# A two-stage mixture-of-experts block: the second stage scatters into the output under an index bound, and its last tile stands under a condition

## The chip, the core and the metric

The kernel runs on one core of a Trainium2 chip. The metric is the device time of one execution in microseconds (us), taken as the median of several runs. All data are 32-bit floats.

## The reference

The input x has 4 batches of 512 rows with 256 columns, 2048 rows in all. Three residual steps follow each other, each on a layer-normalised x:

```python
x = x + 0.5 * ffn(layernorm(x), gate, w0, w1, wo)      # stage one
x = x + attn(layernorm(x), ...)                        # 16 heads, low-rank q and kv, rotary part
x = x + 0.5 * ffn(layernorm(x), gate, w0, w1, wo)      # stage two, the same weights

def ffn(x, gate, w0, w1, wo):                          # 8 experts, the 2 best for each row
    top_w, top_i = top_k(x @ gate, 2)
    combine = one_hot(top_i) weighted by softmax(top_w)
    inter = silu(x @ w0[e]) * (x @ w1[e])              # 256 -> 512, for each expert e
    return sum over e of combine[e] * (inter @ wo[e])  # 512 -> 256
```

So each row goes through two of the eight experts in each stage, and 4096 (row, expert) pairs have to be computed in a stage.

## The kernel before, in words

**Tiles.** The pairs of a stage are sorted by expert into tiles of 128 rows. As the counts are known at run time alone, the number of tiles is the worst case: `NTILES` is 36 for every input. An expert's remainder of at most 64 rows takes half a tile, which it shares with another expert's; the first four places of the second list of tiles (`NSHARED`) can be such shared tiles. Slots that no row fills point at spare rows behind the 2048 real ones, or have weight zero.

**Lists.** A stage's tiles come in two lists that `list_tiles` makes. In stage two the first, `list_a`, has 17 tiles that are certainly full once three of the four batches are routed. The second, `list_b`, has the other 19 and is made after the last batch is routed, while the tiles of `list_a` run. Small matmuls with selection matrices (`sel`) pick out each tile's row numbers (`idx`), weights (`w`) and the offset of its expert in the weight tiles (`off`). `rest_of` lets shared and other tiles alternate for the first eight places, so the tiles 17 to 24 hold four shared tiles, and the tiles 25 to 35 are whole ones.

**One tile** goes through these steps in `ffn_tiles`: `gather` (POOL, indirect DMA) fetches its rows of the normalised x; `turn` transposes them on TensorE (`pt_x`) and copies them (`xT`, DVE); `hidden` loads the expert's offset into a register of TensorE (L1075), multiplies by w0 and w1 (`h`, L1104), takes the silu on ScalarE (`g`) and the product on DVE (`it`); `turn_hidden` transposes that (`pt_i`, `iT`); `project` multiplies by wo (`py`) and scales by the weight on DVE (`yo`, L1176); `scatter` (POOL, L1153) adds the rows of `yo` into DRAM by an indirect DMA that accumulates. The loop runs these one tile apart, so that TensorE has the next tile's product to do while the other engines work; gathers run two to four tiles ahead. Only the last tile has no follower: there the tile before it is projected between the two halves of the last hidden product.

**Scatters.** A row may lie in two tiles, so each scatter waits until the one before has landed. A shared tile scatters each half by itself, the second half one tile later (`later`). Each scatter is one instruction on POOL's queue, in which the gathers stand as well, in the program's order.

**Accumulators.** There are two DRAM tensors, `acc_d[0]` for stage one and `acc_d[1]` for stage two, each with 256 spare rows; POOL's queue clears the spare rows at the start (`clear`). Stage one adds into `acc_d[0]`, which starts as a copy of x. Attention reads it back, batch by batch, and when a batch is done `finish_x` writes it to `acc_d[1]` (SP's queue, L1469). Stage two's tiles 0 to 24 add into `acc_d[1]`. After tile 24 (`final` is 25) SP copies `acc_d[1]` into the output in four DMAs (L1192), which wait for tile 24's scatter; the tiles 25 to 35 add straight into the output. Their scatters wait for the four copies. The first two of them are held back (`HELD`) so that gathers can pass them on POOL's queue.

**Order.** The order of instructions on each engine is the one written in the program (`manual_schedule`); semaphores are put in by what reads and writes what. At the program's end (L1688) each engine drains and they meet at a barrier.

Of the kernel before, what the change touches and what calls it, by code (L numbers as in the profile page):

```python
# [42 lines left out]
def kernel(  # L43
# [64 lines left out]


    xn_d = [dp.tile([NTOK + P, D], F32, name=f"xn_d{f}") for f in range(2)]  # L110
    acc_d = [dp.tile([NTOK + 2 * P, D], F32, name=f"acc_d{f}") for f in range(2)]


    tab_d = [dp.tile([P * P, 2], F32, name=f"tab_d{f}") for f in range(2)]
# [2 lines left out]
    def rows(t, b):  # L117
        return t[b * S : (b + 1) * S, :].rearrange("(t p) d -> p t d", p=P)
# [95 lines left out]
    nc.gpsimd.memset(zero, 0.0)  # L214

    def clear():
        for t in (xn_d[0], acc_d[0], xn_d[1], acc_d[1]):
            for r in range(NTOK, t.shape[0], P):
                nc.gpsimd.dma_start(t[r : r + P, :], zero)
        for t in tab_d:  # L220
            nc.gpsimd.dma_start(t.rearrange("(c s) v -> c (s v)", s=P), zero)
# [656 lines left out]
    def list_tiles(ph, n, m, split=0, read=None):  # L878
# [14 lines left out]
        def parts():  # L893
# [95 lines left out]
            if last:  # L989
                for i, second in enumerate((tab2, ph.tab[:, 1, :HP])):  # L990
                    for r in (slice(0, HP), slice(HP, P)):
                        nc.tensor.matmul(
                            px[r, i, :ns], lhsT=ph.tab[:, i, r], rhs=sel[:, :ns],
                            start=True, stop=(r.start == 0),
                        )
                    nc.tensor.matmul(
                        px[HP:, i, :ns], lhsT=second, rhs=sh[:, 1], start=False, stop=True
                    )
                nc.tensor.matmul(
                    px[:1, 2, n : n + ns], lhsT=e_off, rhs=own, start=True, stop=True  # L1000
                )
            nc.tensor.matmul(
                px[:, 0, n0:n1], lhsT=ph.tab[:, 0, :], rhs=sel[:, n0:n1],
                start=True, stop=True,
# [24 lines left out]
            res["w"] = rt.tile([P, NTILES], F32, tag=f"wt{last}", name="wt")  # L1029
            nc.vector.tensor_copy(res["w"][:, :n], px[:, 1, :n])  # L1030
            res["off"] = rt.tile([1, NTILES], I32, tag=f"off{last}", name="off")
            n2 = n + n0
            nc.vector.tensor_copy(res["off"][:, :n2], px[:1, 2, :n2])
            if last:
                res["off2"] = res["off"][:, n:n2]

        return res, parts()

    HELD = 2
    flat_out = out.rearrange("b s d -> (b s) d")  # L1040

    def ffn_tiles(f, jobs, final=None):
# [2 lines left out]

        n = len(jobs)
        xg, xT, begun = {}, {}, set()

        def gather(j):
# [91 lines left out]
        def turn_hidden(it):  # L1143
# [4 lines left out]
            nc.scalar.copy(iT, pt)  # L1148
            return iT

        def scatter(these):
            for dst, idx, y in these:
                nc.gpsimd.indirect_dma_start(  # L1153
                    out=dst,
                    out_offset=bass.IndirectOffsetOnAxis(ap=idx, axis=0),
                    in_=y,
                    in_offset=None,
                    compute_op=ALU.add,
                )
            these.clear()  # L1160

        def project(j, off, iT):
            res, i = jobs[j]
            py = ps_p.tile([P, D], F32, tag="p", name="py")
            two = shared(j)
            for m in range(MC):
                first_half(two, py, iT[:, m, :], w_sb[2][:, bass.ds(off + m * D, D)], m, MC)
                if two:
                    wo = copies[j][2 * DC + m // 2][:, m % 2 * D : (m % 2 + 1) * D]
                    second_half(py, iT[:, m, :], wo, m, MC)  # L1170
            copies.pop(j, None)
            direct = final is not None and j >= final

            pool, tag = (qp, "q") if direct else (ptp, "pt")
            y = pool.tile([P, D], F32, tag=tag, name="yo")
            nc.vector.tensor_scalar_mul(y, py, res["w"][:, i : i + 1])  # L1176
            two_rows = P if two else 0
            dst = flat_out if direct else acc_d[f][: res["rows"] + two_rows, :]
            idx = res["idx"][:, i : i + 1]
            if two:  # L1180

                held.append((dst, half_idx[:, 0, i : i + 1], y))
                later.append((dst, half_idx[:, 1, i : i + 1], y))
            else:
                held.append((dst, idx, y))
            if not direct or j >= final + HELD:
                scatter(held)
            if final is not None and j == final - 1:

                for r in range(0, NTOK, NTOK // 4):  # L1190
                    r = slice(r, r + NTOK // 4)
                    nc.sync.dma_start(  # L1192
                        flat_out[r, :].rearrange("(p r) d -> p (r d)", p=P),
                        acc_d[f][r, :].rearrange("(p r) d -> p (r d)", p=P),
                    )

        held, later = [], []
        gather(0)
        gather(1)
        yield -1  # L1200
# [3 lines left out]
        for j in range(n):  # L1204
            gather(j + 2)
            if final is not None and j >= final:

                gather(j + 3)
                if j > final:
                    gather(j + 4)  # L1210
            scatter(later)
            if j == n - 1:

                off, it = hidden(j, lambda: project(*todo))
                todo = None
            else:
                off, it = hidden(j)
            yield j
            turn(j + 1)
            yield j  # L1220
            if todo is not None:
                project(*todo)
            yield j
            todo = (j, off, turn_hidden(it))
            yield j
        project(*todo)

# [236 lines left out]
    def finish_x(i):  # L1466
        b, h = items[i]
        if h == NH - 1:
            nc.sync.dma_start(rows(acc_d[1], b), xs[b])  # L1469

    def rest_of(res, n):

# [24 lines left out]
    for half in range(2):  # L1497
# [2 lines left out]

    nc.sync.dma_start(mark_d, list_a["w"][:, :n_a])
    nc.sync.dma_start(
        acc_d[0][:NTOK, :].rearrange("(p r) d -> p (r d)", p=P),
        x.rearrange("b s d -> (b s) d").rearrange("(p r) d -> p (r d)", p=P),
    )
    load_attention()
# [9 lines left out]
    for j in tiles:  # L1516
        place = place + 1 if place < 4 else 1
        beside.at(place)
        if j < n_a - 2:
            beside.step(3)  # L1520
            if j == n_a - 3 and place == 4:
                beside.finish()
        elif j == done + 1 and place == 1:
            load_x(0, rows(acc_d[0], 0))
        elif j == done + 2 and place == 1:
            beside.add(prepare(0), put_queries(0), put_queries(1))
        elif j > done + 2:
            beside.step(2 if place % 2 == 0 else 1)
        if j == len(jobs) - 1:
            if place == 1:  # L1530
                beside.finish()
            put_scores(place - 1)
            put_divide(place - 1)
    load_x(1, rows(acc_d[0], 1))
    for k in range(NT, NT + LEAD):
        put_scores(k)
        put_divide(k)
# [19 lines left out]
    for i, (b, h) in enumerate(items):  # L1557
        if h == 2:
            if b > 0:
                load = None  # L1560
                if b + 1 < B:
                    load = lambda b=b: load_x(b + 1, rows(acc_d[0], b + 1))
                routed = {}
                beside.add(route_one(two, b - 1, routed, load))
            if b + 1 < B:
                beside.add(prepare(b + 1))
            if b > 0:
                beside.add(scatter_one(two, routed))
            if b == B - 1:
                beside.add(listing)  # L1570
        for kc in range(NT):

            at = NT * (h % 2) + kc
            beside.at(at, at in (6, 7, 0, 1), LITTLE if late and ROOM[at] < 1.0 else ROOM[at])
            k = (i + 1) * NT + LEAD + kc
            if at != 1 or i == 0:
                put_scores(k)
            if at == 0 and i > 0:

                put_scores(k + 1)  # L1580
                put_weigh(i - 1, range(NT))
                put_divide(k)
                beside.step(PARTS[at])
            if at == 5:

                put_divide(k - 1)
            pts[i, kc] = turn_probs(probs[i], kc)
            for f in late:
                f()
            late.clear()  # L1590
            if at == 1:
                asked.add(put_queries(i // 2 + 2))
                beside.step(PARTS[at])
            elif at == 4 and h % 4 == 1 and i > 1:
                late.append(put_out(i - 2, 0))
            elif at == 6 and h % 4 == 1 and i > 1:
                late.append(put_out(i - 2, 1))
                late.append(lambda i=i: finish_x(i - 2))
            asked.step(ASKED[at])
            if at == 0 and i == 0:  # L1600
                put_divide(k)
            if at > 1 or at == 0 and i == 0:
                beside.step(PARTS[at])
        probs.pop(i)
# [87 lines left out]
```

## Time and profile before

| what | value |
|---|---|
| median of 3 runs | 1111.03 us (1108.27 to 1111.64) |
| the profiled execution | 1107.51 us, span of its instructions 1105.7 us |
| mean granted TensorE clock | 0.990 of full speed |
| TensorE (PE) busy | 1053.1 us, 95% of the span |
| DVE, ScalarE (ACT), POOL busy | 562.1, 476.5, 586.7 us |
| stage two's scatters | 40: 21 whole and 8 half ones to the accumulator, 11 to the output |
| the four copies to the output | issued from 1040.5 us on, 512 KB each, median 5.6 us to landing |

Times in the profile are counted from the span's first instruction. Busy time leaves out what an engine's sequencer does by itself (waits, register loads, branches, drains). A POOL row for an indirect DMA shows the time of its issue; the transfer goes on after it. A wait for several semaphores is put down to the one that came last, and "issue" means that the profile shows no wait. [...]

### The profile page before, as it was taken

The page shows a single profiled execution, that of the slowest core. Times are in us where ns is not written, and L with a number is a line of the kernel's source. Part 1 is how long each engine was busy: PE and PEld are TensorE (multiplying, and loading weights), DVE is VectorE, ACT ScalarE, POOL GpSimd, SP SyncE. Part 2 cuts the span into 40 slices and gives each one's busy share as a digit, 9 for nine tenths or more (in the row PEclk, how much of TensorE's full clock was granted, in tenths as well). Part 3 has the DMA queues.
Part 4 walks back from the last instruction along what each step waited for, and adds up shares of the span by engine and source line. Part 5 has one row for each costly group of instructions (what it writes and reads, how often), then busy time and mean ns, then how long its engine had stood idle before and what let it go on. Part 6 is the DMA issues. An engine that isn't in the chain of part 4 may idle for free. (4 is left out here: it accounts for less than half of the span.)

```text
span 1105.7 us, 14702 instructions
## 1 busy us (share of the span) xinstructions
PE 1053.1 (95%) x4738; PEld 598.2 (54%) x4738; DVE 562.1 (51%) x1329; ACT 476.5 (43%) x1030; POOL 586.7 (53%) x655
## 2 busy tenths in 40 slices
PE   4899999999999999999999999999999899999994
PEld 3566555666545555455455545554555566655662
DVE  6563222334566565676666766666855342322221
ACT  3622432222555556545565554556545231144120
POOL 4345455466556555536774546864574247444442
PEclk8999999999999999999999999999999999999998
DMA  9973233322100000100000100001000224223422
GB/s 315 366 189 48 45 49 52 67 34 39 34 1 1 1 1 1 58 1 1 1 2 20 39 1 1 1 1 39 2 6 1 86 50 45 45 48 53 129 44 24
DMA packets 44043, 53.57 MB, mean 48 GB/s; under 512 B 10720, under 2 KB 36704, under 8 KB 43872
## 3 DMA queue, kind: packets, MB, share of 16 engines
q0 software_dynamic: 16960, 22.07, 12.6%
q1 hardware_dynamic: 26736, 30.55, 8.6%
q8 instruction: 40, 0.66, 0.2%
q14 instruction: 35, 0.29, 0.1%
q10 hardware_dynamic: 272, 0.01, 0.0%
HBM read 34.74 MB, written 22.07 MB: 51 GB/s over the span
## 5 line engine op out<-in xcount | busy, mean ns | idle before, releaser
L1104 PE MATMUL h<-w_sb,xT 128*128 (+1 forms) x576 | 260.3, 594 | 2.5 <-DVE xT L1072 1.9
L1355 PE MATMUL ps<-k,q 128*128 128x512 f32 x512 | 259.8, 600 | 0.8 <-ACT pr L1365 0.8
L1363 DVE TENSOR_REDUCE nm<-ps 128x1 f32<-128x512 f32 x256 | 175.0, 687 | 74.6 <-PE ps L1355 70.1
L1365 ACT ACTIVATE pr<-ps,nm 128x512 f32<-128x512 f32 x210 | 144.2, 687 | 129.0 <-DVE nm L1363 101.7
L1372 POOL TENSOR_SCALAR pr<-pr,sm 128x512 f32<-128x512 f32 x210 | 142.4, 694 | 69.8 <-DVE sm L1370 68.5
L1140 DVE TENSOR_TENSOR it<-g,h 128x512 f32<-128x512 f32 x72 | 49.5, 688 | 221.2 <-PE h L1104 174.6
L1104 PEld LDWEIGHTS h<-w_sb,xT 128*128 128x128 f32 (+1 forms) x576 | 100.4, 184 | 109.6 <-issue 103.4
L1378 PEld LDWEIGHTS pt<-ident,pr 128*128 128x128 f32 x840 | 102.9, 141 | 103.7 <-issue 64.8
L1153 POOL DMA_INDIRECT acc_d<-yo,idx x53 | 83.9, 1582 | 140.3 <-DVE yo L1176 73.7
L1148 ACT COPY iT<-pt_i 128x512 f32<-128x512 f32 x72 | 42.3, 587 | 246.0 <-PE pt_i L1146 246.0
L1378 PE MATMUL pt<-ident,pr 128*128 128x128 f32 x840 | 135.5, 275 | 4.2 <-ACT pT L1385 3.8
L1104 PE MATMUL py<-w_sb,iT 128*128 (+1 forms) x576 | 136.9, 381 | 1.4 <-ACT iT L1148 1.4
L1391 PE MATMUL po<-pT,low 128*64 128x512 f32 x512 | 116.9, 598 | 4.7 <-ACT pr L1365 4.6
L1383 DVE COPY pT<-pt 128x512 f32<-128x512 f32 x128 | 87.4, 683 | 55.0 <-PE pt L1378 55.0
L1241 POOL TENSOR_TENSOR tsin<-tsin,sin_sb 128x512 f32<-128x512 f32 x36 | 46.5, 1293 | 126.1 <-DVE tsin L1239 123.9
L1104 PEld LDWEIGHTS py<-w_sb,iT 128*128 128x128 f32 (+1 forms) x576 | 100.5, 184 | 18.2 <-ACT iT L1148 2.4
L1355 PEld LDWEIGHTS ps<-k,q 128*128 128x128 f32 x512 | 82.4, 190 | 44.1 <-issue 19.4
L1057 POOL DMA_INDIRECT xg<-xn_d,idx x72 | 72.4, 1006 | 30.1 <-issue 15.6
L1385 ACT COPY pT<-pt 128x512 f32<-128x512 f32 x128 | 74.1, 579 | 15.3 <-PE pt L1378 15.3
L1391 PEld LDWEIGHTS po<-pT,low 128*64 128x64 f32 x512 | 33.9, 136 | 83.5 <-issue 56.5
L1137 ACT ACTIVATE g<-h 128x512 f32<-128x512 f32 x72 | 43.0, 597 | 59.2 <-PE h L1104 56.2
L1176 DVE TENSOR_SCALAR yo<-py,wt 128x256 f32<-128x256 f32 x72 | 34.8, 483 | 63.6 <-PE py L1104 55.4
(234 smaller groups left out, 1329.2 us busy)
## 6 DMA issues: line engine op xcount, KB each, us to landing
w_sb<-in_L_ffn_w_kernel_dram SPq DMA_DIRECT2D x8, 1024.0 KB, 13.7
w_sb<-in_L_ffn_wo_kernel_dram SPq DMA_DIRECT2D x5, 1024.0 KB, 14.5
xn_d<-xn SPq DMA_DIRECT2D x12, 256.0 KB, 4.3
x<-_attn_hidden_states_dram SPq DMA_DIRECT2D x4, 512.0 KB, 10.1
x<-acc_d SPq DMA_DIRECT2D x4, 512.0 KB, 3.9
acc_d<-x SPq DMA_DIRECT2D x4, 512.0 KB, 3.0
out_dram<-acc_d SPq DMA_DIRECT2D x4, 512.0 KB, 5.6
xg<-xn_d,idx POOLq DMA_INDIRECT x72, 2.8
```

The lines of the kernel that those rows point to most:

```text
L1057: nc.gpsimd.indirect_dma_start(out=xg[j], out_offset=None, in_=xn_d[f][: res["rows"], :], in_offset=bass.IndirectOffsetOnAxis(ap=res["idx" ...
L1104: nc.tensor.matmul(to[r], lhsT=lhsT[:, r], rhs=rhs, start=(k == 0), stop=(k == last - 1))
L1140: nc.vector.tensor_mul(it, g, ph[1])
L1153: nc.gpsimd.indirect_dma_start(out=dst, out_offset=bass.IndirectOffsetOnAxis(ap=idx, axis=0), in_=y, in_offset=None, compute_op=ALU.add,)
L1355: nc.tensor.matmul(ps, lhsT=qT[:, t * P : (t + 1) * P], rhs=st[b]["k"][h % 2], start=True, stop=True,)
L1363: nc.vector.tensor_reduce(nm, ps, AX.X, ALU.max, negate=True)
L1365: nc.scalar.activation(pr, ps, AF.Exp, bias=nm, accum_out=sm[:, t : t + 1])
L1372: nc.gpsimd.tensor_scalar(pr, pr, sm[:, t : t + 1], 1.0, ALU.mult, ALU.mult)
L1378: nc.tensor.transpose(pt[:, t * P : (t + 1) * P], probs[t][:, kc * P : (kc + 1) * P], ident)
L1383: nc.vector.tensor_copy(s, pt)
L1385: nc.scalar.copy(s, pt)
L1391: nc.tensor.matmul(po[j * RANK : (j + 1) * RANK], lhsT=st[b]["low"][:, kc, 1, :], rhs=pts[j], start=(kc == 0), stop=(kc == NT - 1),)
```

## The change

Stage two adds to the output from its first tile on. `finish_x` writes each finished batch to the output, `acc_d[1]` is gone with its clears, and so are the four copies and the holding back of scatters. As the output has no spare rows, every scatter of stage two carries a bound on the index: a row number above 2047 is left out and is no error. The loop runs over 35 tiles. The 36th, the last place of `list_b`, follows under a condition: one more matmul in `list_tiles` adds up the last column of `sel`, which is 1 if that place has rows and 0 if not, and the result stands in `off`'s row as one more element (`used`). After its last instruction of tile 34 each of the five engines loads `used` into a register and branches. In the branch that is taken when it is 0, an engine only brings the semaphores to the counts that the left-out tile would have given them. The matmul is there in both stages' `list_b`; the condition in stage two alone.

```diff
-    acc_d = [dp.tile([NTOK + 2 * P, D], F32, name=f"acc_d{f}") for f in range(2)]
+    acc_d = dp.tile([NTOK + 2 * P, D], F32, name="acc_d")
...
     def clear():
-        for t in (xn_d[0], acc_d[0], xn_d[1], acc_d[1]):
+        for t in (xn_d[0], acc_d, xn_d[1]):
...
+                nc.tensor.matmul(
+                    px[:1, 2, n + ns : n + ns + 1], lhsT=ones[:, :1], rhs=sel[:, n - 1 :],
+                    start=True, stop=True,
+                )
...
-            n2 = n + n0
+            n2 = n + n0 + (1 if last else 0)
             nc.vector.tensor_copy(res["off"][:, :n2], px[:1, 2, :n2])
             if last:
-                res["off2"] = res["off"][:, n:n2]
+                res["off2"] = res["off"][:, n : n2 - 1]
+                res["used"] = res["off"][:, n2 - 1 : n2]
...
     def ffn_tiles(f, jobs, final=None):
-        n = len(jobs)
+        n = len(jobs) - (0 if final is None else 1)
...
+        skip = {"bounds_check": NTOK - 1, "oob_is_err": False} if f else {}
+
         def scatter(these):
             for dst, idx, y in these:
                 nc.gpsimd.indirect_dma_start(
...
                     compute_op=ALU.add,
+                    **skip,
                 )
...
-            dst = flat_out if direct else acc_d[f][: res["rows"] + two_rows, :]
-            idx = res["idx"][:, i : i + 1]
+            dst = flat_out if f else acc_d[: res["rows"] + two_rows, :]
             if two:
-                held.append((dst, half_idx[:, 0, i : i + 1], y))
+                scatter([(dst, half_idx[:, 0, i : i + 1], y)])
                 later.append((dst, half_idx[:, 1, i : i + 1], y))
             else:
-                held.append((dst, idx, y))
-            if not direct or j >= final + HELD:
-                scatter(held)
-            if final is not None and j == final - 1:
-                for r in range(0, NTOK, NTOK // 4):
-                    r = slice(r, r + NTOK // 4)
-                    nc.sync.dma_start(
-                        flat_out[r, :].rearrange("(p r) d -> p (r d)", p=P),
-                        acc_d[f][r, :].rearrange("(p r) d -> p (r d)", p=P),
-                    )
+                scatter([(dst, res["idx"][:, i : i + 1], y)])
...
         project(*todo)
+        if final is not None:
+            used = nc.values_load(
+                jobs[n][0]["used"], min_val=0, max_val=1,
+                skip_runtime_bounds_check_because="a sum of zeros and at most a one",
+            )
+            with tc.If(used > 0):
+                n += 1
+                gather(n - 1)
+                turn(n - 1)
+                off, it = hidden(n - 1)
+                project(n - 1, off, turn_hidden(it))
...
     def finish_x(i):
         b, h = items[i]
         if h == NH - 1:
-            nc.sync.dma_start(rows(acc_d[1], b), xs[b])
+            nc.sync.dma_start(rows(flat_out, b), xs[b])
```

More of the change, by code (lines that the diff above doesn't have):

```diff
@@ L1031, in parts @@
             res["off"] = rt.tile([1, NTILES], I32, tag=f"off{last}", name="off")
-            n2 = n + n0
+            n2 = n + n0 + (1 if last else 0)
             nc.vector.tensor_copy(res["off"][:, :n2], px[:1, 2, :n2])
             if last:
-                res["off2"] = res["off"][:, n:n2]
+                res["off2"] = res["off"][:, n : n2 - 1]
+                res["used"] = res["off"][:, n2 - 1 : n2]
         return res, parts()
-    HELD = 2
     flat_out = out.rearrange("b s d -> (b s) d")
     def ffn_tiles(f, jobs, final=None):
-        n = len(jobs)
+        n = len(jobs) - (0 if final is None else 1)
         xg, xT, begun = {}, {}, set()
@@ L1171, in project @@
             copies.pop(j, None)
-            direct = final is not None and j >= final
-            pool, tag = (qp, "q") if direct else (ptp, "pt")
+            pool, tag = (qp, "q") if final is not None and j >= final else (ptp, "pt")
             y = pool.tile([P, D], F32, tag=tag, name="yo")
@@ L1177, in project @@
             two_rows = P if two else 0
-            dst = flat_out if direct else acc_d[f][: res["rows"] + two_rows, :]
-            idx = res["idx"][:, i : i + 1]
+            dst = flat_out if f else acc_d[: res["rows"] + two_rows, :]
             if two:
-                held.append((dst, half_idx[:, 0, i : i + 1], y))
+                scatter([(dst, half_idx[:, 0, i : i + 1], y)])
                 later.append((dst, half_idx[:, 1, i : i + 1], y))
             else:
-                held.append((dst, idx, y))
-            if not direct or j >= final + HELD:
-                scatter(held)
-            if final is not None and j == final - 1:
-                for r in range(0, NTOK, NTOK // 4):
-                    r = slice(r, r + NTOK // 4)
-                    nc.sync.dma_start(
-                        flat_out[r, :].rearrange("(p r) d -> p (r d)", p=P),
-                        acc_d[f][r, :].rearrange("(p r) d -> p (r d)", p=P),
-                    )
-        held, later = [], []
+                scatter([(dst, res["idx"][:, i : i + 1], y)])
+        later = []
         gather(0)
@@ L1502 @@
     nc.sync.dma_start(
-        acc_d[0][:NTOK, :].rearrange("(p r) d -> p (r d)", p=P),
+        acc_d[:NTOK, :].rearrange("(p r) d -> p (r d)", p=P),
         x.rearrange("b s d -> (b s) d").rearrange("(p r) d -> p (r d)", p=P),
@@ L1523 @@
         elif j == done + 1 and place == 1:
-            load_x(0, rows(acc_d[0], 0))
+            load_x(0, rows(acc_d, 0))
         elif j == done + 2 and place == 1:
@@ L1533 @@
             put_divide(place - 1)
-    load_x(1, rows(acc_d[0], 1))
+    load_x(1, rows(acc_d, 1))
     for k in range(NT, NT + LEAD):
@@ L1561 @@
                 if b + 1 < B:
-                    load = lambda b=b: load_x(b + 1, rows(acc_d[0], b + 1))
+                    load = lambda b=b: load_x(b + 1, rows(acc_d, b + 1))
                 routed = {}
```

## The prediction, made before the changed kernel ran

> **What bounds the kernel now.** I read the page first: its span, the busy shares and the 40 slices.
>
> ```profile
> span 1105.7 us, 14702 instructions
> ...
> PE 1053.1 (95%) x4738; PEld 598.2 (54%) x4738; DVE 562.1 (51%) x1329; ACT 476.5 (43%) x1030; POOL 586.7 (53%) x655
> ...
> PE   4899999999999999999999999999999899999994
> ```
>
> TensorE is busy in every slice but the first and the last, so in the body only PE work that is removed counts. The last slice reads 4: something else sets the end there. The timeline of the last 36 us shows it (columns: start, duration, engine, line, operation; in brackets the idle time before, and what ended it):
>
> ```profile
> 1083.20 0.48 DVE L1176 TENSOR_SCALAR yo<-py,wt 128x256 f32<-128x256 f32 x1 [0.87 <-PE py L1104]
> ...
> 1083.42 1.55 POOL L1153 DMA_INDIRECT out_dram<-yo,idx  x1 [3.31 <-issue]
> ...
> 1087.08 0.48 DVE L1176 TENSOR_SCALAR yo<-py,wt 128x256 f32<-128x256 f32 x1 [3.40 <-PE py L1104]
> ...
> 1087.95 1.55 POOL L1153 DMA_INDIRECT out_dram<-yo,idx  x1 [2.97 <-DVE yo L1176]
> ...
> 1092.43 1.55 POOL L1153 DMA_INDIRECT out_dram<-yo,idx  x1 [2.93 <-DMA out_dram<-yo,idx]
> 1092.96 0.48 DVE L1176 TENSOR_SCALAR yo<-py,wt 128x256 f32<-128x256 f32 x1 [3.42 <-PE py L1104]
> 1097.02 1.55 POOL L1153 DMA_INDIRECT out_dram<-yo,idx  x1 [3.03 <-issue]
> ```
>
> The last `yo` row is tile 35's; counting backwards, the scatter at 1092.43 is tile 34's, whose `yo` was done at 1087.56, and tile 35's own, ready at 1093.44, starts at 1097.02. The scatters run 4.5 us apart (1.55 of issue, 2.9 until the one before has landed) and are late. Where they fell behind stands some 45 us earlier, in the timeline from 1036 us on:
>
> ```profile
> 1036.63 1.59 POOL L1153 DMA_INDIRECT acc_d<-yo,idx  x1 [2.85 <-DVE xT L1072]
> ...
> 1040.53 2.45 SPq L1192 DMA_DIRECT2D out_dram<-acc_d  x4
> ...
> 1051.30 1.61 POOL L1153 DMA_INDIRECT out_dram<-yo,idx  x1 [7.96 <-issue]
> ```
>
> 1036.63 is tile 24's scatter, itself late (its `yo` was done at 1031.3). The four copies wait for it, and tile 25's scatter waits for the copies: 14.7 us in the place of 4.5. It and the ten after it run at 4.5 us against 5.82 us a tile; they never quite catch up. The line of the program's end, asked for its rows (count, shortest/median/longest ns), shows what follows:
>
> ```profile
> L1688 POOLq DRAIN  x3: 46/107/8082, 1096.8 to 1105.4; - x3
> ```
>
> POOL's drain of 8.08 us starts with the last scatter and ends 7.9 us after it; from the last scatter's start to the span's end is 1105.7 - 1097.02 = 8.68 us. The loads of a register from a tile, in the same columns:
>
> ```profile
> L1075 PEldq TENSOR_LOAD <-off x72: 295/302/719, 46.2 to 1082.1; - x72
> L1075 ACTq TENSOR_LOAD <-off x8: 277/282/469, 106.4 to 1007.1; - x8
> ```
>
> **Which way the condition falls.** The 36 tiles are a worst case. Counting the reference's own top-2 choices on its inputs, the second stage's experts get 485, 449, 435, 575, 543, 551, 506 and 552 rows: 28 full tiles of 128, three remainders over 64 with a tile each, five of at most 64 in three shared tiles. That is 34, so tiles 34 and 35 of 0..35 are empty; the change drops 35. It would take two more tiles to fill it; one choice that falls otherwise by rounding moves the count by one at most.
>
> **The change part by part.**
>
> 1. *Tile 35 goes.* Tile 34 becomes the last and takes the last tile's order of work. The `yo` rows 1071.56, 1077.38, 1083.20 lie 5.82 us apart, so the last `yo` ends at 1092.96 + 0.48 - 5.82 = 1087.62.
>
> 2. *Two new 1x1 matmuls* (one in each stage's last list, on PE's path). Nearest row: the one-row product with e_off, next start 0.12 to 0.14 us later. 2 x 0.12 = 0.24; last `yo` done at 1087.86. The copy to `off` grows by one element: nothing, as the four copies of 9 to 31 elements all take 0.15 to 0.17 us.
>
> 3. *The copies and the hold go.* Scatter 25 then follows scatter 24 by 4.5 us: 1041.1, then 1045.6, 1050.1, 1054.6; tile 28's `yo` is done at 1054.6, so there the backlog ends, and from tile 29 each scatter follows its own `yo` by 0.28 us (first tile of the stage: `yo` done 883.91, scatter 884.19). Two gathers between two scatters (1.3 us each) fit into the 2.9 us of landing. Last scatter: 1087.86 + 0.28 = 1088.14. Scatter 33 starts near 1082.0, lands after 3.8 and is out of the way. Steps 1 to 3 bring the last scatter from 1097.02 to 1088.14: 8.9 us, of which 5.8 are the tile and 3.3 the backlog, less 0.24.
>
> 4. *Load and branch on each engine, after its last instruction.* PE, DVE, ACT and SP reach it before POOL's drain ends, with 7 us and more to spare: nothing, and if that cover were gone, 0.4 us. On POOL, behind the last scatter: a register load (0.30 by PE's row, 0.28 by ACT's), a compare and branch, a wait on two DMAs that landed tiles before, a semaphore instruction for the two DMAs left out, a branch. No row shows a branch or that instruction; between the 0.02 us of a POOL semaphore wait and the 1.55 us of a scatter's issue, I take 0.1, nearest the short sequencer rows (drains of 0.05 and 0.11, a semaphore clear of 0.16). If the drain's end hangs on the scatter, all of it is hidden: 0. If the drain takes its 8.08 us from wherever it starts, the sum is at most 0.9. I take 0.4. [...]
>
>    The profile page's part on DMA queues has the row `q8 instruction: 40, 0.66, 0.2%`: code comes by DMA, 40 packets of 16.5 KB, 0.66 MB for 14702 instructions or some 45 bytes each. The branch jumps over three instructions of POOL and some forty of PE, a ninth of a packet at most. A jump to code that isn't there yet would cost between 0 and a small DMA's landing, 2.7 us (nwq's row); I take 0 and keep 2.7 for the range.
>
>    [...]
>
> 5. *Bound on the index, on all of stage two's scatters.* Before's scatters have none. Rows of POOL's indirect DMAs: gather 1.00, scatter-add 1.58 us; the gap to the plainer kind, 0.58, is the nearest price of more work per row, so the bound may cost -0.1 (rows left out) to +0.6 each. I take 0: the issue takes 1.57 to 1.58 us whichever target and index list it has. What is free: from 988.90 (first half scatter) to 1088.14 are 21 intervals, 99.2 us; the chain needs 47.7 for the first 11 (to 1036.63) and 10 x 4.5 = 45. The 6.5 us left over are 0.31 us a scatter.
>
> 6. *x goes to out instead of the accumulator; the first scatter waits for the last batch's write as well.* That write issues at 871.20 and lands in 3.0; the first scatter is at 884.19, cover 10 us. Queued behind that wait on POOL: the gathers of tiles 3 on. Nothing; without the cover, what it is late by.
>
> 7. *Two clears fewer at the start* (0.54 us of POOL each near 12.9). POOL's next compute at 24.20 sat idle 5.16 us before it, for DVE: 0, at most a gain of 1.1.
>
> **Sum.** End of span: 1088.14 + 8.68 + 0.4 = 1097.2, against 1105.7: 8.5 us less. The profiled execution took 1107.51 in all, 1.8 us around its span and 3.5 us under the median of the runs, 1111.03 (1108.27 to 1111.64). I carry the difference to the median: 1111.03 - 8.5 = 1102.5.
>
> **Rivals.**
>
> *The bounded scatter is slower, and POOL's chain becomes the bound.* Place: the 21 intervals of step 5. Up to 0.31 us a scatter it costs nothing; each 0.1 us beyond moves the end 2.1 us. The gain is gone at 0.31 + 8.5/21 = 0.71 us. With 1.1 us (between the 0.58 gap and a second pass of 1.58): 21 x 0.79 = 16.6 later than the forecast, 1119. With 0.58 it is 5.7 later, 1108.2. For it: the 4.5 us cadence has little slack. Against: the even issue times of step 5, and spare rows drop out. 9%.
>
> *The end costs more than the scatter's shift.* A code fetch on POOL, or a drain that starts later: 2.7 + 0.9 - 0.4 = 3.2 on top, 1105.7. For it: a drain whose 7.9 us nothing in the trace explains (the scatter itself landed after 3.7). 13%.
>
> *The tile is not skipped* (used comes out as 1). It would then run without overlap behind the branch: gather 1.0 + 2.8 landing, transposes and copies 2.4, products 3.6 + 1.9, the hidden product's tail 1.4, `yo` 0.5, sum 13.6 from 1090.0; scatter near 1103.9, end 1112.6: 6.9 later than before, 1117.9. Against: the counts above. 3%.
>
> **How the numbers follow.** The forecast has 75%, its own range 1099 to 1105 (the three runs of before spread by 3.4 us). The range to both sides: down to 1098 if the difference is taken from the profiled run's lower level or the clears give 1.1 us; up to 1107, which takes in the second rival and half of the small prices of the first. Outside lie the rest of the first rival and the third. A measurement of this kernel can tell about 0.3%, 3.3 us, from no change. Faster needs under 1107.7: the forecast, and most of the second rival, 0.84; same 0.06 (the first rival at prices near 0.58, the tail of the second); slower 0.10 (the rest of the first, and the third).
>
> **What would show it.** Right: 35 `yo` rows in stage two; no copies from the accumulator; scatters of tiles 29 to 34 within 0.4 us of their `yo`; the last one near 1088, the span's end 8.7 to 9.1 us behind it; PE's pace still 5.82 us. Step 5 is wrong if the issue of a bounded scatter is over 1.6 us, or the interval over 4.5. Step 4 is wrong if POOL idles between the branch and its drain, or the drain ends over 9 us after the last scatter. The forecast falls if a 36th `yo` appears, or if PE waits for a gather held up on POOL.

## The result, and the profile after

The changed kernel takes 1101.03 us, the median of six runs (1099.24 to 1103.48), and the kernel before took 1110.34 us beside it (six runs, 1108.27 to 1112.62). The ratio is 0.9913, 95% interval 0.9901 to 0.9925: faster by 9.3 us. The forecast was 1102.5 us, 8.5 us less. The profiled execution of the changed kernel took 1100.0 us in all.

The page of the changed kernel, its span, busy shares and TensorE's 40 slices:

```profile
span 1098.2 us, 14690 instructions
...
PE 1047.2 (95%) x4720; PEld 594.0 (54%) x4720; DVE 560.4 (51%) x1326; ACT 475.3 (43%) x1028; POOL 581.6 (53%) x651
...
PE   4899999999999999999999999999999899999995
```

TensorE has 5.9 us less work and still fills every slice but the ends. The timeline of the last stretch shows who comes last (start, duration, engine, line, operation; in brackets the idle time before and what ended it; `yo` is now L1185, the scatter L1162):

```profile
1078.71 0.48 DVE L1185 TENSOR_SCALAR yo<-py,wt 128x256 f32<-128x256 f32 x1 [0.87 <-PE py L1110]
1079.47 1.55 POOL L1162 DMA_INDIRECT out_dram<-yo,idx  x1 [4.27 <-DVE yo L1185]
1082.59 0.48 DVE L1185 TENSOR_SCALAR yo<-py,wt 128x256 f32<-128x256 f32 x1 [3.40 <-PE py L1110]
1083.99 1.55 POOL L1162 DMA_INDIRECT out_dram<-yo,idx  x1 [2.97 <-DMA out_dram<-yo,idx]
1088.47 0.48 DVE L1185 TENSOR_SCALAR yo<-py,wt 128x256 f32<-128x256 f32 x1 [3.42 <-PE py L1110]
1089.23 1.55 POOL L1162 DMA_INDIRECT out_dram<-yo,idx  x1 [3.69 <-DVE yo L1185]
```

The last `yo`, now tile 34's, ends at 1088.95 and its scatter starts 0.28 us later; before, the last scatter started 3.58 us behind its `yo`. Only the last but one (1083.99) still waits for another scatter, as its `yo` comes 3.88 us after the one before (1082.59 against 1078.71), and scatters that follow each other here start 4.5 us apart. POOL's timeline from tile 24 on shows where the backlog goes:

```profile
1036.68 1.59 POOL L1162 DMA_INDIRECT out_dram<-yo,idx  x1 [2.63 <-issue]
...
1041.31 1.60 POOL L1162 DMA_INDIRECT out_dram<-yo,idx  x1 [0.43 <-issue]
...
1045.85 1.58 POOL L1162 DMA_INDIRECT out_dram<-yo,idx  x1 [1.65 <-issue]
...
1050.50 1.58 POOL L1162 DMA_INDIRECT out_dram<-yo,idx  x1 [1.77 <-DVE yo L1185]
```

Tile 24's scatter is late, as before (its `yo` ended at 1032.63). Then the chain gains 1.2 to 1.3 us a tile: 4.6 between scatters against 5.82 between `yo`. From tile 27 on the bracket names `yo` and no longer a landing or POOL's own work: the chain has caught up.

The end, by the rows of the branch's lines on POOL's sequencer (shortest, median, longest ns; first and last start) and of the program's end:

```profile
L1225 POOLq TENSOR_LOAD <-off x1: 508/508/508, 1089.0 to 1089.0; - x1
...
L1229 POOLq COMPARE_BRANCH  x1: 53/53/53, 1089.6 to 1089.6; - x1
...
L1229 POOLq INC_SWDGE_SEM  x1: 1595/1595/1595, 1089.8 to 1089.8; - x1
...
L1696 POOLq DRAIN  x3: 46/107/5872, 1091.5 to 1097.9; - x3
```

The load and the branch run while the last scatter is still being issued (1089.23 to 1090.78): the sequencer runs ahead of it. The semaphore instruction for the DMAs left out (INC_SWDGE_SEM) is long, and ends 0.65 us after the issue. The drain follows. From the last scatter's start to the span's end it is 8.94 us; it was 8.67. Before has an instruction of that name at the program's start alone, and there it is short:

```profile
L1675 POOLq INC_SWDGE_SEM  x1: 31/31/31, 0.1 to 0.1; - x1
```

### The profile page after: what moved, and what is told of

Same layout as the page of the kernel before. It is cut to its first block, busy times and chain, and to the rows that moved or that the text cites. A ratio compares the mean times of both kernels' runs of the same rounds, so it can differ in the third digit from the quotient of the medians.

```text
span 1098.2 us, 14690 instructions
## 1 busy us (share of the span) xinstructions
PE 1047.2 (95%) x4720; PEld 594.0 (54%) x4720; DVE 560.4 (51%) x1326; ACT 475.3 (43%) x1028; POOL 581.6 (53%) x651
## 5 line engine op out<-in xcount | busy, mean ns | idle before, releaser
L1110 PE MATMUL h<-w_sb,xT 128*128 (+1 forms) x568 | 256.8, 594 | 2.5 <-DVE xT L1078 1.9
L1162 POOL DMA_INDIRECT acc_d<-yo,idx x32 | 50.5, 1577 | 83.6 <-DVE yo L1185 37.3
L1162 POOL DMA_INDIRECT out_dram<-yo,idx x31 | 49.2, 1586 | 85.7 <-DVE yo L1185 60.5
```

Source lines behind the costliest of these rows:

```text
L1110: nc.tensor.matmul(to[r], lhsT=lhsT[:, r], rhs=rhs, start=(k == 0), stop=(k == last - 1))
L1162: nc.gpsimd.indirect_dma_start(out=dst, out_offset=bass.IndirectOffsetOnAxis(ap=idx, axis=0), in_=y, in_offset=None, compute_op=ALU.add, * ...
```

## The experiments

The whole time differs by a few us from one execution of a kernel to the next, mostly by stage one (last experiment), so each edit is read in its profile from a fixed point: from the start of tile 24's `yo`, just before the copies of before, to the end of the span. The two starts, before and after:

```profile
1030.82 0.48 DVE L1176 TENSOR_SCALAR yo<-py,wt 128x256 f32<-128x256 f32 x1 [0.86 <-PE py L1104]
```

```profile
1032.15 0.48 DVE L1185 TENSOR_SCALAR yo<-py,wt 128x256 f32<-128x256 f32 x1 [0.85 <-PE py L1110]
```

This stretch leaves out whatever an edit costs ahead of tile 24, and each is read from one profile. "Lag" is from the last `yo`'s end to the last scatter's start, "tail" from there to the span's end.

| kernel | tile 24's `yo` to end, us | against before | lag | tail |
|---|---|---|---|---|
| before | 74.87 | | 3.58 | 8.67 |
| changed | 66.02 | -8.85 | 0.28 | 8.94 |
| changed, run again | 66.04 | -8.83 | 0.27 | 8.95 |
| 36 tiles, no condition | 71.53 | -3.34 | 0.27 | 8.63 |
| condition alone | 71.85 | -3.02 | 5.90 | 9.15 |
| always 35, no branch | 65.65 | -9.22 | 0.28 | 8.57 |
| condition's body runs | 82.02 | +7.15 | 0.27 | 8.72 |
| no bound on the index | 66.30 | -8.57 | 0.28 | 9.22 |
| clears kept | 66.20 | -8.67 | 0.28 | 9.12 |
| two tiles under the condition | 60.34 | -14.53 | 0.47 | 8.88 |

**The direct adds without the condition.** All 36 tiles run.

```diff
-        n = len(jobs) - (0 if final is None else 1)
+        n = len(jobs)
...
-        if final is not None:
-            used = nc.values_load(
...
-            with tc.If(used > 0):
-                n += 1
-                gather(n - 1)
...
```

> The change without its condition: all 36 tiles in the loop, adds straight to the output with the bound. My theory: the condition is worth one tile's pace, so the last yo comes 5.82 us after the changed kernel's (1088.47 + 5.82 = 1094.3), its scatter follows by 0.28 us, and the span ends 8.7 us after that scatter, near 1103.7: 5.5 us more than the changed kernel's 1098.2, and some 2 to 3.5 us less than before's median. Rival, the load and branch cost several us that the drain does not hide: then taking them away gives back 2 us or more, and the span ends near 1101.5.

The stretch is 3.34 us shorter than before, and the lag falls from 3.58 to 0.27. So the copies and the hold were worth 3.3 us with the tile still there. The median is 1109.36 against 1109.69 us (ratio 0.9992, 0.9969 to 1.0014), where I had expected 2 to 3.5 us less than before: the stretch shows the 3.3 us and the whole time doesn't. The interval, -3.4 to +1.6 us, just takes them in; whether something ahead of tile 24 eats them up stays open.

**The condition without the direct adds.** The second accumulator, the copies and the hold stay; 35 tiles and the branch. The lines show what it has beyond the changed kernel.

```diff
+    acc_d = [dp.tile([NTOK + 2 * P, D], F32, name=f"acc_d{f}") for f in range(2)]
...
+                held.append((dst, idx, y))
+            if not direct or j >= final + HELD:
+                scatter(held)
+            if final is not None and j == final - 1:
+                for r in range(0, NTOK, NTOK // 4):
+                    r = slice(r, r + NTOK // 4)
+                    nc.sync.dma_start(
...
```

> The kernel before with the condition alone: accumulator, four copies and held scatters stay. My theory: here the last scatter hangs on the chain of scatters behind the copies and not on its tile, so dropping a tile takes one interval of 4.5 us off the end and not a tile's 5.82; tile 34's scatter starts near 1092.5 and the span ends 9.0 us behind it, near 1101.5 to 1102.5: some 4 us less than before's median. Rival, the tile's time is what counts: 5.8 us less.

POOL's timeline of this kernel:

```profile
1038.57 1.59 POOL L1158 DMA_INDIRECT acc_d<-yo,idx  x1 [2.98 <-issue]
...
1053.33 1.61 POOL L1158 DMA_INDIRECT out_dram<-yo,idx  x1 [8.06 <-DMA out_dram<-acc_d]
...
1095.25 1.55 POOL L1158 DMA_INDIRECT out_dram<-yo,idx  x1 [3.02 <-issue]
```

The hole of 14.76 us at the copies is back (8.06 of it waited for `out_dram<-acc_d`), and the last `yo`, at 1089.35, is 5.90 us ahead of its scatter. A tile of 5.82 us is gone from TensorE, but the end was hanging on the scatters, and there one tile fewer is one interval: 3.02 us in all, 4.57 for the interval, less 1.1 by which this execution's scatters started and ran later and 0.5 of longer tail. The time is 1106.64 us, ratio 0.9971 (0.9952 to 0.9990). The two parts alone give 3.3 and 3.0 us, together 8.85: the tile counts in full only when the scatters have caught up.

**No branch at all.** Stage two always runs 35 tiles; the load, the condition and its body are taken out.

```diff
-        if final is not None:
-            used = nc.values_load(
...
-            with tc.If(used > 0):
-                n += 1
-                gather(n - 1)
...
```

> The changed kernel without load and branch: the loop simply ends after 35 tiles (tile 35, which is empty on these inputs, is left out for good). My theory: POOL's drain hangs on the last scatter, so only the 0.3 us go by which the end came later after it (8.97 against 8.68): 0.3 us less than the changed kernel. Rival, load, branch and the semaphore instruction of 1.6 us lie on the path: 2.2 to 2.5 us less.

> The changed kernel again, as the measure for the three runs beside it. All theories: some 9 us under before's median; if the 1.3 us by which TensorE fell behind before its last tiles in the first profile come from the change, they are there again at the same places (near 92, 820 and 925 us); if they are chance, they lie elsewhere or are gone.

The stretch is 65.65 us, with the branch 66.02 and 66.04: the branch costs 0.38 us, and 0.37 of that is the tail (8.57 against 8.94). Over the table the tail is 8.88 to 9.22 with the branch skipped and 8.57 to 8.72 in the other four, so the cost is 0.4 us to within some 0.2. The changed kernel run again beside it gives 1105.39 against 1113.88 us, ratio 0.9923 (0.9903 to 0.9943). The kernel without the branch has 1108.17 us (0.9944, 0.9922 to 0.9965), 2.8 us more than with it. In the two profiles that difference (1106.3 against 1103.9 of span) lies ahead of the branch, 2.2 us of it in stage one; it is taken up below.

**The condition's body runs.** The comparison is turned round, so that tile 35 is computed behind the branch.

```diff
-            with tc.If(used > 0):
+            with tc.If(used < 1):
```

> The changed kernel with the condition turned round (used < 1), so that the last tile, which is empty here, runs behind the branch without overlap. My theory, from the third rival's sum: 13.6 us from the gather's issue to yo done, and the gather is issued 1.8 us after the last scatter in the loop starts: yo done near 1104.6, scatter 1104.9, span's end 1113.6, 15.4 us more than the changed kernel. Rival, the branch's code has to be fetched first: 2.7 us or more on top, with an idle stretch after the branch on PE or POOL.

Its last stretch:

```profile
1095.44 1.55 POOL L1162 DMA_INDIRECT out_dram<-yo,idx  x1 [3.70 <-DVE yo L1185]
1097.30 1.02 POOL L1063 DMA_INDIRECT xg<-xn_d,idx  x1 [0.31 <-issue]
...
1100.17 0.66 PE L1075 MATMUL pt_x<-ident,xg 128*128 128x128 f32 x2 [5.52 <-DMA xg<-xn_d,idx]
...
1101.35 5.30 PE L1110 MATMUL h<-w_sb,xT 128*128 x8 [0.52 <-DVE xT L1078]
...
1111.65 1.58 POOL L1162 DMA_INDIRECT out_dram<-yo,idx  x1 [13.33 <-DVE yo L1185]
```

From the gather to the end of `yo` (1111.38) it is 14.1 us, where the third rival worked out 13.6; from scatter to scatter 16.2. The stretch is 16.0 us longer than with the tile skipped and 7.15 longer than before (the rival said 6.9); the time is 1118.84 us, 1.0074 (1.0048 to 1.0100). The gather starts 0.31 us after tile 34's scatter, the usual gap on POOL (0.30 between a scatter and the gather behind it in the changed kernel): entering the body cost POOL no wait for code. What the rival had too small is `h`, 5.30 us for 3.6; its other terms were 1.2 us too large together. TensorE had idled 5.52 us for the gather, and its clock was low afterwards, as these two stretches show (busy us per engine, then the granted clock):

```profile
1100.00:1105.00 5.00, 4.32 (x7) 1.99 (x8) 0.42 (x1) 0.04 (x1) 0.00 (x0) 0.54 0.00 0
1105.00:1112.00 7.00, 4.30 (x16) 2.24 (x14) 1.17 (x2) 1.15 (x2) 0.34 (x1) 1.00 0.00 0
```

In stretches of half a microsecond the granted clock is 0.50 from 1098.0 to 1104.5 us and 1.00 from 1105.0 on.

**No bound on the index.** Stage two adds to a second accumulator with spare rows instead, without the bound.

```diff
+    acc2_d = dp.tile([NTOK + 2 * P, D], F32, name="acc2_d")
...
-        skip = {"bounds_check": NTOK - 1, "oob_is_err": False} if f else {}
+        skip = {}
...
-            dst = flat_out if f else acc_d[: res["rows"] + two_rows, :]
+            dst = (acc2_d if f else acc_d)[: res["rows"] + two_rows, :]
```

> The changed kernel with stage two's scatters going to a second accumulator with spare rows, without the bound; finish_x writes each batch to both, and the accumulator is never copied out, so the second stage's part is missing from the output. My theory: the bound costs nothing: issue 1.55 to 1.64 us and 4.5 us between late scatters in both, the time as the changed kernel's within 0.5 us. Rival, the bound costs 0.1 us or more a scatter: the issue, or the interval between late scatters, is shorter here by that, and the backlog ends one tile sooner.

The scatters' rows, the changed kernel's with the bound first, then all of this kernel's without:

```profile
L1162 POOL DMA_INDIRECT out_dram<-yo,idx x31: 1552/1586/1638, 885.1 to 1089.2; - x31
```

```profile
L1163 POOL DMA_INDIRECT acc_d<-yo,idx x63: 1547/1583/1639, 64.2 to 1096.5; - x63
```

1586 and 1583 ns, late scatters 4.5 to 4.7 us apart in both, and a stretch of 66.30 for 66.02, whose 0.28 lies in the tail: the bound costs nothing that can be read. The time is 1107.50 us (0.9950, 0.9931 to 0.9968).

**The two clears kept.** A spare tile's rows are cleared at the start in the place of the second accumulator's.

```diff
+    rest_d = dp.tile([NTOK + 2 * P, D], F32, name="rest_d")
...
-        for t in (xn_d[0], acc_d, xn_d[1]):
+        for t in (xn_d[0], acc_d, xn_d[1], rest_d):
```

> The changed kernel with the two clears at the start kept (of a tensor that nothing reads). My theory: they lie in POOL's idle time: 0 us. Rival, they take POOL's time or the DMA's at the start: up to 1.1 us more, and the first yo of stage one comes 0.4 us later, where before had it (61.38 against 60.95).

1103.12 us, ratio 0.9911 (0.9892 to 0.9930), beside 0.9923 of the changed kernel on the same chip, and the first `yo` of stage one comes at 60.58 us, not later than without them (60.95): the clears are worth nothing that can be read.

**Two tiles under the condition.** Tile 34 joins tile 35 there, and `used` asks for the last but one place.

```diff
-                    px[:1, 2, n + ns : n + ns + 1], lhsT=ones[:, :1], rhs=sel[:, n - 1 :],
+                    px[:1, 2, n + ns : n + ns + 1], lhsT=ones[:, :1], rhs=sel[:, n - 2 : n - 1],
...
-        n = len(jobs) - (0 if final is None else 1)
+        n = len(jobs) - (0 if final is None else 2)
...
-                n += 1
-                gather(n - 1)
-                turn(n - 1)
...
+                n += 2
+                for j in (n - 2, n - 1):
+                    gather(j)
+                for j in (n - 2, n - 1):
+                    turn(j)
...
```

> The changed kernel with its last two tiles (34 and 35, both empty on these inputs) under one condition on the first of them; the loop has 34 tiles. My theory: one more tile's pace off the end, 5.8 us: last scatter near 1083.4, span's end 9.0 us behind it, near 1092.4, some 14.5 us under before's median. Rival, the end is held by something other than the last tile (the chain of scatters, which had caught up by tile 28 or 29, or the drain): less than 4 us.

The stretch is 5.68 us shorter than the changed kernel's: another tile's pace of 5.82 us, less 0.19 of longer lag, with 0.06 of shorter tail. The time is 1097.21 us, ratio 0.9879 (0.9852 to 0.9906), the fastest of all kernels here. The inputs need 34 tiles, so a third would have to run in the body.

**What the end hangs on.** By the rows of before and after, POOL's drain ended 7.9 and 8.1 us after the last scatter's start, though its row began 0.2 us ahead of that start in the one and 2.2 us behind it in the other, so I took it to hang on the scatter. Three kernels tried that, with small power operations behind the last scatter that nothing needs, two and eight of them with the branch, eight without.

```diff
         if final is not None:
+            for _ in range(2):        # 8 in the second and the third
+                nc.gpsimd.tensor_tensor(spin, ones[:, :8], power, ALU.pow)
             used = nc.values_load(
```

> The changed kernel with two small power operations on POOL put behind the last scatter, ahead of the register load, into a tile of their own that nothing reads. Each takes about 1.65 us by the rows of the same operation on 128x8, so POOL comes to its closing drain some 3.3 us later. If the drain's end hangs on the scatter (it came 7.9 us after the scatter's start before the change and 8.1 after it, though it started 1.7 us further behind the scatter after it), the drain gets shorter by 3.3 us and from the last scatter's start to the span's end it stays 8.9 us, within 0.3. Rival: the drain takes its 5.9 us from wherever it starts; then the distance is 12.2 us.

> The same with eight of the operations, some 13.2 us of POOL behind the last scatter, so that the drain starts when the scatter has long landed. If the drain's end hangs on the scatter, the drain itself takes under 0.5 us here, and the span ends about 13.2 + 1.55 (the scatter's issue) + 2.2 (load, branch, semaphore instruction) + 1.0 (what follows the drain) = 17.9 us after the last scatter's start. Rival: the drain keeps 5.9 us wherever it starts; then it is 23 us.

> Stage two always runs 35 tiles, with no load, no branch and no semaphore instruction, and eight small power operations (some 14.2 us) stand on POOL behind the last scatter. It parts what the two runs before left open: there a drain that started 5.8 us and 16.0 us after the last scatter's start still took 5.872 us, but a semaphore instruction of 1.6 us stood just ahead of it. If any closing drain of POOL takes some 6 us from where it starts, the last scatter's start to the span's end is about 1.0 + 14.25 + 6.0 + 0.85 = 22 us. Rival: it was the semaphore instruction that the drain waited for, and without it the drain hangs on the scatter alone, long landed; then the drain is under 0.5 us and the distance some 16.5 us.

The two operations and the drain behind them, the drain behind eight, and the eight and the drain without the branch:

```profile
1096.08 3.96 POOL L1227 TENSOR_TENSOR spin<-ones,power 128x8 f32<-128x8 f32 x2
```

```profile
L1699 POOLq DRAIN  x3: 46/107/5872, 1100.8 to 1107.3; - x3
```

```profile
L1699 POOLq DRAIN  x3: 46/107/5872, 1107.6 to 1114.1; - x3
```

```profile
1094.13 14.25 POOL L1227 TENSOR_TENSOR spin<-ones,power 128x8 f32<-128x8 f32 x8
```

```profile
L1689 POOLq DRAIN  x3: 46/107/7565, 1106.7 to 1114.8; - x3
```

My theory fell. The drain takes 5.872 us whether it starts 5.8 or 16 us behind the last scatter, and the tails are 12.48 and 22.76 us. Nor does it hang on the semaphore instruction: without one, the drain ends 5.89 us after the last operation (1094.13 + 14.25 = 1108.38 to 1114.28), and the tail is 21.96. So POOL's last work, whichever of the three kinds tried here, is followed by a drain of about six us: 6.3 after the end of the last scatter's issue in the kernel before (1098.57 to 1104.88), 5.87 after the semaphore instruction in the changed one. One run each: 1109.39, 1116.12 and 1116.91 us. What fills the six us stays open.

**Why medians and stretches disagree.** Stage one, from the first tile's `yo` to the last, takes 227.8 us in the profile of before and 228.1 after; 232.6 in the changed kernel run again, and 234.8 and 233.9 in the kernels without branch and without bound. TensorE's rows near 99 us show part of it, the changed kernel first, then the same kernel run again:

```profile
97.37 0.28 PE L993 MATMUL px<-sel,tab 128*64 128x4 f32 x4 [0.98 <-DVE tab L554]
...
99.30 1.89 PE L1110 MATMUL py<-w_sb,iT 128*128 x8
```

```profile
99.44 0.28 PE L993 MATMUL px<-sel,tab 128*64 128x4 f32 x4 [3.30 <-DVE tab L554]
...
101.57 3.23 PE L1110 MATMUL py<-w_sb,iT 128*128 x8
```

TensorE waited 3.30 us, instead of 0.98, for a table that comes back by DMA (DVE had waited 6.30 us for `tabr<-tab_d` before it wrote `tab`), and the eight products took 3.23 us instead of 1.89. From 100 to 150 us the first has a granted clock of 1.00, and the second this (busy us per engine, granted clock, DMA share, GB/s):

```profile
100.00:150.00 50.00, 50.00 (x231) 28.58 (x229) 12.50 (x29) 19.95 (x37) 22.15 (x17) 0.97 0.31 48
```

In stretches of half a microsecond the clock is 0.50 from 101.0 to 104.0 us, with the edges 3.4 us at half rate. Of the 4.5 us by which the second's stage one is longer, this can cost 1.7 at most, half of the 3.4, and the longer wait cost 2.3. The profiles of before, after, the 36 tiles and the condition alone have none there. The other kernels have one, of 3.4 us or (two tiles under the condition, two operations) of 6.8, and some a second near 50 or 183 us. The length of the one wait doesn't decide: 2.15 us was followed by none (36 tiles), 1.49 by one (no bound). As one and the same kernel fell on both sides, the edit alone doesn't decide it either. Waits and half rate together move an execution by some us, and the twelve runs of the 36 tiles lie between 1105.95 and 1115.96. What triggers it was not separated further.

## Why the prediction was right, step by step

1. **Tile 35 goes, 5.82 us.** 35 `yo` rows, a pace of 5.82 still. Against the 36 tiles the condition brought 5.51 us (71.53 to 66.02), which is 5.82 less 0.31 of longer tail. Right.
2. **Two 1x1 matmuls, 0.24 us.** The trace has the first at 98.22 us and the product after it at 98.33: 0.11 us. Right in size; too small to be read in the total.
3. **Copies and hold, 3.3 us.** 3.34 by the 36 tiles. The scatters caught up at tile 27, a tile earlier than said, and each later one but the last but one follows its `yo` by 0.28 us. That one, tile 33's, was to be within 0.4 us and is 0.92 late (1083.07 to 1083.99): the working had overlooked that its `yo` follows tile 32's by 3.88 us, less than the 4.5 of a scatter. The last scatter starts 5.24 us later and isn't held, so the sum is right.
4. **Load and branch, 0.4 us.** 0.38 measured, but by luck and not by the working. POOL's register load takes 0.51 us where 0.30 was taken. The semaphore instruction that I put at 0.1 us takes 1.595, about the upper bound that I had; the "at most 0.9" left that bound out. "No row shows that instruction" was a slip as well, for before has one at the program's start. The drain does not hang on the scatter but comes after whatever POOL did last. That the cost stayed small is the sequencer's doing: it starts the load 0.2 us ahead of the last scatter's issue and the semaphore instruction 0.95 us ahead of the issue's end, so only 0.65 us of all of it stands behind the scatter, and the drain is 0.3 to 0.4 shorter there. The code fetch at 0 held as far as the rows show: on ScalarE, DVE and POOL the next instruction starts 0.14 to 0.23 us after the branch's end. On TensorE it starts 1.0 us after, when tile 34's last product, for which it waits, is done; a fetch shorter than that would not show. A branch over more than these some forty of TensorE's instructions was not tried. The compare-and-branch, for which the prediction had no row, took 45 ns on ScalarE, 53 on POOL, 72 on DVE and 230 on TensorE in the changed kernel.
5. **The bound on the index, 0.** 1586 ns against 1583. Right; with it falls the first rival, whose whole price it was.
6. **The first scatter's wait, 0.** It starts at 885.1, 0.3 us after its `yo`, as before. Right.
7. **Two clears, 0.** Right.

The tail was given as 8.7 to 9.1 us: 8.94. The second rival had the right mechanism, a drain that starts later, but 0.3 us of it and not 0.9, and no fetch that shows.

**The sum.** The profiled spans differ by 7.5 us, less than the 8.5 forecast (the end is at 1098.2, forecast 1097.2), since the changed execution came 1.33 us late to tile 24 (1032.15 against 1030.82). Most of that is one wait of TensorE in attention, near 820 us, for a `q` that POOL computes. The changed kernel run again has it too:

```profile
821.07 1.13 PE L1363 MATMUL ps<-k,q 128*128 128x512 f32 x2 [1.19 <-POOL q L1251]
```

```profile
825.92 1.12 PE L1363 MATMUL ps<-k,q 128*128 128x512 f32 x2 [1.34 <-POOL q L1251]
```

Before has no such wait. POOL idles 1.64 us ahead of this `q` in both kernels with the second accumulator and 2.25 to 4.64 us in the eleven profiles with the direct adds, and in seven of these TensorE waits for it, 0.55 to 1.34 us. So this wait goes with the direct adds, and the prediction has no term for it; what holds POOL there stays open. Two smaller waits of the first profile, 0.77 us near 92 us and 0.21 near 925, are not there in the second. The medians differ by 9.3 us here, and by 8.5 in the second comparison, and can't tell a microsecond. The rest of the sum fits the stretch: -5.82 - 3.34 + 0.31 = -8.85, as measured.

## What to carry to other kernels

Ask of each saving what is last at the end: here a tile of 5.8 us taken from TensorE alone brought 3.0 us, as a chain of scatters stood behind it, and taking away that chain's hole brought 3.3 alone and let the tile count in full. A condition on each engine around the work that an input seldom needs cost 0.4 us when skipped and 16 when run, so by my estimate it pays as long as that tile is needed less often than about one time in three (5.5 gained against some 10.5 lost, by the stretches of the 36 tiles, the changed kernel and the body that runs). Read a change of under 1% in a fixed stretch of the trace, beside the whole time, and look ahead of the stretch for waits that the edit brings.

## What the runs showed of the hardware that was not expected

- POOL's closing drain ends 5.7 to 6.3 us after its last work, a scatter, a semaphore instruction or a compute operation alike; work put behind the last scatter moves the end by nearly its whole length (3.96 us moved the tail by 3.5, 14.25 by 13.8).
- POOL's sequencer runs ahead: its register load began 0.23 us before the scatter in front of it was issued.
- INC_SWDGE_SEM took 1.6 us behind a scatter and behind power operations, as long as a scatter's issue, but 0.03 us at the program's start; why is open. A register load from a tile took 0.28 us on ScalarE, 0.30 on TensorE, 0.51 on POOL and 0.55 on DVE.
- TensorE's half-rate stretches of 3.4 or 6.8 us came in some executions of a kernel and not in others, behind single waits as short as 1.2 us (1.19 with eight operations and the branch); the trace doesn't show why.
